# Query rotations, quantizer blocks and the last norm moved within a decoder kernel's order of work

## The chip, the cores and the metric

The kernel runs on one core of a Trainium2 chip. Its time is the device time of one execution in microseconds; the number used is the median of several executions. A core has a TensorE (PE) for matrix products and transposes, a VectorE (DVE), a ScalarE (ACT) and a GpSimd (POOL) for element-wise work, and SyncE (SP), which here only issues transfers. Each engine works through its own queue of instructions in order and waits on semaphores for what other engines produce. Data lies in on-chip SBUF; TensorE writes into PSUM, from which VectorE or ScalarE read.

## The reference

Two batches of 512 tokens, width 1024, with a context of 1024 rows each, go through two layers, each of an attention-like part and a feed-forward part. All is f32 except the first product, which is of integers.

```python
x = x + L0_xattn(layernorm(x), ctx)    # fake_quant(x) @ fake_quant(ctx): round, clip to 0..255
x = x + L0_ffn(layernorm(x))           # x @ W.T + b, plus LoRA terms weighted by a router's softmax
x = x + L1_xattn(layernorm(x), ctx)    # 32 query heads, 8 key/value heads of 128; rotary q and k;
                                       # softmax(q k / sqrt(128) + mask) v, then @ wo
x = x + L1_ffn(layernorm(x))           # x @ W_up.T, plus the LoRA term of the top-1 expert
```

The rotation of a query or a key is `q * cos + rotate_half(q) * sin`, where `rotate_half` swaps the two halves of the 128 channels with a sign. The top-1 expert is found by `argmax` over four logits.

## The kernel before

**Products.** Every large matrix product is split into two by two blocks and made from seven block products instead of eight (`seven` and `seven_onto`, L340 for their matmuls). The sums of blocks that this needs are made by `left_sums` and `right_sums` (L238 to L260), mostly on VectorE. A product of the seven is four or eight matmuls into one PSUM bank; it is then added to others (L277 copies the first on ScalarE; L281 to L293 add on VectorE; for sums onto x L308 to L315, with POOL doing L315). These functions are generators: one step is one block product.

**Order.** TensorE's instructions run in the order in which the program writes them. Other engines' instructions are ordered by a scheduler, except in hand-ordered regions: the very start on VectorE, and, from the first attention step to almost the last, VectorE, ScalarE and POOL. In the tail the scheduler orders them again. Buffers come from pools of 14, 17 and 10 slots of 8, 4 and 2 KB a partition (`u8`, `u4`, `u2`), with 2 wide PSUM buffers and 4 of one bank (`b`). Transfers are issued mostly from SP's queue, those of rows and some of the context from ScalarE's, constants from POOL's.

**First stage: keys and values, with the quantized product between.** For each batch, keys (two stages) and values (two stages) of 14 block products each are the main work. `quantized_product` (from L389 on) is woven in at every second block product (`weave`, called at L1035): it loads and quantizes eight context blocks two at a time, then for each of four row blocks of x makes the norm (L168, L175, L176), quantizes it (L193 to L197), and turns the block before it with eight bf16 transposes (`turned`, L406), evacuated by L158 or on ScalarE. Then come column sums (L427) and the four integer products (L441), evacuated by L449 and L451. Keys are rotated by `rope` (L210 to L216).

**Middle.** The first layer's linear part with its router, and the norm of x (`query_norm`, with transposes L203 evacuated by L204 and L205). Then the queries, eight stages of 14 block products; finished and rotated queries are stored to memory (`q_d`). The last stage's 14 products are not run at once: they are handed to attention as `extra["products"]`, spread over its first steps (3, 2, 2, 2, 2, 2, 1 at steps n = -2 to 4). Eight query heads come out of them. In this stage the list `later` collects whole rotations, and a step runs them at its end.

**Attention.** `attention` runs over n from -2; a step handles three heads in three stages of their life, and has three stretches. In the first the newest head's scores are made (L737, four pairs of matmuls into the wide buffers, evacuated with the mask added by L751 into `e`). In the second come the block products of the output projection of a former group, or the extra products, interleaved with the maximum tree of the newest head (L759 to L765). In the third, the middle head gets its maximum spread (L779), is reduced by it (L783), goes through the exponential (L786), and POOL sums it (L789 to L794); the oldest head is multiplied with the values (L800, copied by L808); and maxima and sums are turned by `over_partitions` (L701 transposes, L703 reduction, L774 reciprocal) and sent through memory to become rows (L710, L716). A head's output is divided by its sum on POOL (L811, in the next step).

**Tail.** During the last steps the moments of the first batch are taken (`all_moments`: L163, L164, square root L186, reciprocal L187), then that batch is normed and turned (`normed`, L168 and L203), the gate and the LoRA's inner product are made (`gated`: L929, the choice of the expert L940 to L952, transposes L962 and copy L963, L577), and the last linear layer runs (`linear`), first for batch 0 beside the last projection, then for batch 1. Its weight is loaded by L543 in four parts of 1 MB.

The lines that the change touches are L187, `rope`, the end of `quantized_product`, `finish` and `emit` in `queries`, the second and third stretch of `attention`, the `weave` of L1035 and the tail from L1128 on.

Of the kernel before, what the change touches and what calls it, by code (L numbers as in the profile page):

```python
# [31 lines left out]
NT = S // P  # L32
# [3 lines left out]
ATT_SCALE = float(np.float32(1.0) / np.sqrt(np.float32(DH)))  # L36
# [3 lines left out]
def decoder_kernel(  # L40
# [41 lines left out]
    def u4(shape, dtype=F32):  # L82
        return new(shape, "u4", 17, dtype)

    def u2(shape, dtype=F32):
        return new(shape, "u2", 10, dtype)
# [30 lines left out]
    for name, ap in qparams.items():  # L117
        t = const.tile([P, 1], F32, name=f"qp_{name}")
        nc.gpsimd.dma_start(t, ap.partition_broadcast(P))
        qp[name] = t  # L120
    for side in ("x1", "x2"):
        t = const.tile([P, 1], F32, name=f"qp_inv_{side}")
# [56 lines left out]
    def all_moments(b):  # L179

        mv, ready = small([P, NT, 2]), []
        for t in range(NT):
            moments(rows(b, t), mv[:, t, :])
            yield ready
        rstd = small([P, NT])
        nc.scalar.activation(rstd, mv[:, :, 1], AF.Sqrt, bias=eps_t)  # L186
        nc.vector.reciprocal(rstd, rstd)  # L187
        ready += [(mv[:, t, 0:1], rstd[:, t : t + 1]) for t in range(NT)]
        yield ready
# [16 lines left out]

    def rope(dst, acc, half, scale):

        rot = u2([P, HALF])
        nc.scalar.activation(rot[0:64, :], acc[64:128, :], AF.Copy, scale=scale)  # L210
        nc.scalar.activation(rot[64:128, :], acc[0:64, :], AF.Copy, scale=scale)
        nc.vector.scalar_tensor_tensor(
            dst, acc, scale, cos_t[half], ALU.mult, ALU.mult
        )
        nc.vector.tensor_tensor(rot, rot, sin_t[half], ALU.mult)
        nc.vector.tensor_tensor(dst, dst, rot, ALU.add)  # L216
# [111 lines left out]
    def weave(main, side, every, skip=0):  # L328

        for i, _ in enumerate(main):  # L330
            if i >= skip and (i - skip) % every == 0:
                next(side, None)

    def advance(stretches, n):
        for _ in range(n):
            next(stretches)
# [52 lines left out]
    def quantized_product(b):  # L389
        x[b] = halves()  # L390
        for t in range(NT):
            nc.sync.dma_start(rows(b, t), x_in[b, ts(t, P), :])
        q2 = [u8([P, 4, D], BF16) for _ in range(2)]
        for k in range(NKT):
            c_t = u4([P, D])
            nc.sync.dma_start(c_t, ctx_in[b, ts(k, P), :])
            quantized(q2[k // 4][:, k % 4, :], c_t, "x2")
            if k % 2:
                yield
        x1T = u8([P, NC, S], BF16)  # L400
        rsum, l1s = [], []

        def turned(t):
            tr = ps_wide().bitcast(BF16)[:, 0 : NC * P].rearrange("p (c n) -> p c n", c=NC)
            for c in range(NC):
                nc.tensor.transpose(tr[:, c, :], l1s[t][:, ts(c, P)], ident_b)  # L406
            copy_out(x1T[:, :, ts(t, P)], tr)

        for t in range(NT):
            h = layernorm(rows(b, t))  # L410
            l1 = u2([P, D], BF16)
            quantized(l1, h, "x1")
            r = small([P, 1])
            nc.scalar.activation(h, l1, AF.Copy, accum_out=r)
            nc.vector.tensor_scalar(r, r, c_x2, None, ALU.mult)
            rsum.append(r)
            l1s.append(l1)
            if t:
                turned(t - 1)
            yield  # L420
        turned(NT - 1)


        cs = ps_wide()
        for n in range(2):
            for k in range(NKT):
                nc.tensor.matmul(  # L427
                    cs[:, ts(n, HALF)],
                    ones_b,
                    q2[k // 4][:, k % 4, ts(n, HALF)],  # L430
                    start=(k == 0),
                    stop=(k == NKT - 1),
                )
        csum = u4([P, D])
        nc.vector.tensor_scalar(csum, cs, kc2, c_x1, ALU.add, ALU.mult)
        yield
        for t in range(NT):
            acc = ps_wide()
            for n in range(2):
                for c in range(NC):  # L440
                    nc.tensor.matmul(  # L441
                        acc[:, ts(n, HALF)],
                        x1T[:, c, ts(t, P)],
                        q2[c // 4][:, c % 4, ts(n, HALF)],
                        start=(c == 0),
                        stop=(c == NC - 1),
                    )
            y = u4([P, D])
            nc.vector.scalar_tensor_tensor(y, acc, rsum[t], csum, ALU.add, ALU.add)  # L449
            xs = rows(b, t)  # L450
            nc.vector.scalar_tensor_tensor(xs, y, s12, xs, ALU.mult, ALU.add)  # L451
            yield
# [187 lines left out]
    def queries(q, h_ops, w, later=None):  # L640

        def head(m):
            def product(i, acc, start):
                accumulate(
                    acc,
                    [(w[i - 1][:, c, ts(m, P)], h_ops[i - 1][:, c, :]) for c in range(4)],
                    start,
                )

            def finish(i, j, src):  # L650
                dst = u2([P, HALF]) if (i, j) == (0, 0) else src
                rope(dst, src, 0, ATT_SCALE)
                nc.sync.dma_start(q_d[j][4 * q + 2 * i + m], dst)

            def emit(i, j, src):
                if later is None:
                    finish(i, j, src)
                else:
                    later.append(lambda: finish(i, j, src))

            return seven(product, emit)

        return head(0), head(1)
# [161 lines left out]
    def attention(extra):  # L825
# [23 lines left out]
        for n in range(-2, total + GRP + 1):  # L849
# [27 lines left out]
            tree = new.tree() if new else iter(())  # L877
# [12 lines left out]
                next(tree, None)  # L890
            if n == GRP:
                w_ops = {i: output_operand(0, i) for i in (1, 6, 2, 7, 5, 4, 3)}
            for _ in tree:
                pass
            yield

            if mid:
# [13 lines left out]
                new.nmx = from_row(new.nmx)  # L911
            if old:
                old.attend(1)
            for act in extra["later"]:
                act()
            extra["later"].clear()
            yield


# [104 lines left out]
    side = chain(quantized_product(0), quantized_product(1))  # L1024
    for b in range(B):
        if b == 1:
            ctx_raw = [context_quarter(1, ch, kh, nc.scalar) for ch in range(2) for kh in range(2)]
            w = quad_weights(wk, 0)
            ctx_ops = context_sums(ctx_raw)
        for i, stage in enumerate((keys, keys, values, values)):  # L1030
            if b == 0 and i < 2:
                main = chain(*first[i])
            else:
                main = pair(*stage(b, i % 2, ctx_ops, w))
            weave(main, side, 2, 6 if b == 0 and i == 0 else 0)  # L1035
            if i < 3 and (b, i) != (0, 0):
                w = quad_weights((wk, wv)[(i + 1) // 2], (i + 1) % 2)
            if i == 1 and b == 1:
                for _ in side:
                    pass  # L1040
                ab_t = u8([P, 2, D])
                a_t, b_t = ab_t[:, 0].rearrange("p (c m) -> p c m", c=NC), ab_t[:, 1]
                nc.sync.dma_start(a_t, a0T.rearrange("(c p) m -> p c m", p=P))
                nc.gpsimd.dma_start(b_t, b0.partition_broadcast(P))  # L1044
                tT = [None] * B
                hs, steps = normed(0, u8, 2)
                side = chain(steps, routed(0, hs, a_t, b_t, tT))
# [35 lines left out]
    side = query_norm(1)  # L1083
# [29 lines left out]
    with tc.manual_schedule(  # L1113
        engines={
            mybir.EngineType.DVE,
            mybir.EngineType.Activation,
            mybir.EngineType.Pool,
        }
    ):
        for _ in range(3 * (B * NH - 5)):  # L1120
            next(steps)
        stats = all_moments(0)
        for _ in range(NT):
            for _ in range(2):
                next(steps)
            ready = next(stats)
            next(steps)
        next(stats)  # L1128
        for _ in range(3):
            next(steps)  # L1130

    hs, norms = normed(0, u4, 4, ready)
    for _ in range(6):
        next(norms, None)
        next(steps)
    gates = gated(hs)
    next(gates)
    for _ in range(2):
        next(steps)
    bl_t = u4([P, D])  # L1140
    nc.sync.dma_start(bl_t, bl1T)
    w_ops = matrix(wupT, u8, 4)
    zTs = [None, None]
    main = linear(0, token_sums(hs, lambda: u4([P, 4, 256])), w_ops, lambda: zTs[0], bl_t)
    advance(main, 2)
    zTs[0] = next(gates)
    advance(main, 2)
    for _ in range(3):
        next(steps)
    advance(main, 3)  # L1150
# [88 lines left out]
```

## Time and profile before

| | before |
|---|---|
| median of 3 executions | 2557.05 us (2554.49 to 2557.13) |
| the profiled execution | 2557.93 us |
| its span (first to last instruction) | 2556.2 us |
| mean granted TensorE clock | 0.979 |
| TensorE busy | 2455.1 us, 96% |
| VectorE busy | 1858.0 us, 73% |
| POOL busy | 997.6 us, 39% |
| ScalarE busy | 527.9 us, 21% |

The profile is of one execution. A group is named by its line, its engine, and its output and input buffers. A wait is written as the waiting line, an arrow, and the line that ended the wait. In a timeline a row has its start, its duration, the engine and line, and in brackets the idle time ahead of it with what ended it. A window row has the stretch, its length, and for each engine the busy time and the number of instructions, then the granted clock, the share of the transfer engines, and GB/s. One f32 matmul leaves two records.

### The profile page before, as it was taken

Reading aid. Unit: us, or ns where it says so; the run is one execution under the profiler, and the core shown is the slowest. Engines: PE = TensorE matmul, PEld = TensorE weight load, DVE = VectorE, ACT = ScalarE, POOL = GpSimd, SP = SyncE. Lnnn points to the kernel's source line nnn. Section 1 sums busy time; section 2 is a strip of 40 time slices with the busy share of each in tenths; the row PEclk is TensorE's granted clock in tenths of the full one; section 3 lists DMA queues with packets and bytes.
Section 4 is the critical chain, followed back from the end, with each engine's and each line's share of the span. In section 5 each row is a group of like instructions: output and inputs, shape, how many; then the busy total and the mean of one; then the engine's idle time right before and its main releaser. Section 6 shows DMA issues by size and latency. Waiting matters only on the chain. (4 is left out here: it accounts for less than half of the span.)

```text
span 2556.2 us, 19686 instructions
## 1 busy us (share of the span) xinstructions
PE 2455.1 (96%) x6848; PEld 1224.6 (48%) x6856; DVE 1858.0 (73%) x2036; ACT 527.9 (21%) x615; POOL 997.6 (39%) x536
## 2 busy tenths in 40 slices
PE   7999999999999997779999999999999999998998
PEld 3467458654444443334444444444444444444553
DVE  5848764346876555778888888888888888887542
ACT  1301121001222222122222222222222222222000
POOL 0000010110000001354767676767767676766221
PEclk8999999999999998889999999999999999999999
DMA  7325232013893221232343223442233224321300
GB/s 265 113 70 198 103 102 96 21 66 123 317 334 126 86 96 48 68 111 78 79 111 111 75 81 105 136 133 81 87 111 111 75 86 111 111 73 52 124 33 33
DMA packets 147379, 277.54 MB, mean 109 GB/s; under 512 B 29200, under 2 KB 47136, under 8 KB 146256
## 3 DMA queue, kind: packets, MB, share of 16 engines
q1 hardware_dynamic: 107024, 235.96, 28.0%
q10 hardware_dynamic: 39824, 39.60, 6.3%
q8 instruction: 55, 0.90, 0.2%
q0 software_dynamic: 432, 0.71, 0.1%
q14 instruction: 44, 0.36, 0.0%
HBM read 217.24 MB, written 58.98 MB: 108 GB/s over the span
## 5 line engine op out<-in xcount | busy, mean ns | idle before, releaser
L340 PE MATMUL b<-u,u 128*128 128x512 f32 (+1 forms) x3648 | 1415.5, 545 | 24.6 <-DVE u L284 9.6
L340 PEld LDWEIGHTS b<-u,u 128*128 128x128 f32 x3648 | 693.9, 192 | 710.9 <-issue 622.1
L737 PE MATMUL wide<-u,u 128*128 128x512 f32 x1024 | 469.7, 611 | 60.5 <-DVE u L751 58.6
L789 POOL TENSOR_TENSOR u<-u 128x1024 f32<-128x1024 f32 x64 | 151.6, 2368 | 796.3 <-ACT u L786 796.3
L800 PE MATMUL b<-u,u 128*128 128x512 f32 x1024 | 460.3, 592 | 0.0
L751 DVE TENSOR_TENSOR u<-wide,u 128x1024 f32<-128x1024 f32 x256 | 312.3, 1223 | 145.9 <-PE wide L737 145.9
L786 ACT ACTIVATE u<-u 128x2048 f32<-128x2048 f32 x128 | 244.6, 1911 | 788.6 <-DVE u L783 715.6
L737 PEld LDWEIGHTS wide<-u,u 128*128 128x128 f32 x1024 | 199.2, 196 | 319.6 <-issue 187.5
L783 DVE TENSOR_TENSOR u<-u,b 128x2048 f32<-128x2048 f32 x128 | 290.1, 2266 | 0.0
L800 PEld LDWEIGHTS b<-u,u 128*128 128x128 f32 x1024 | 186.2, 192 | 184.6 <-issue 184.6
L315 POOL TENSOR_TENSOR u<-u,u 128x512 f32<-128x512 f32 x120 | 186.9, 1577 | 223.4 <-DVE u L313 208.8
L313 DVE TENSOR_TENSOR u<-u,b 128x512 f32<-128x512 f32 x200 | 135.8, 679 | 135.3 <-PE b L340 135.2
L792 POOL TENSOR_TENSOR u<-u,u 128x1024 f32<-128x1024 f32 x64 | 150.8, 2356 | 37.7 <-ACT u L786 37.5
L793 POOL TENSOR_TENSOR u<-u,u 128x1024 f32<-128x1024 f32 x64 | 152.9, 2389 | 5.0
L811 POOL TENSOR_TENSOR u<-u,u 128x512 f32<-128x512 f32 x64 | 112.5, 1758 | 14.1 <-DMA u<-row 14.1
L1044 POOL DMA_DIRECT2D u<-in_b_dram x1 | 0.6, 561 | 287.5 <-PE wide L441 287.5
L759 DVE TENSOR_TENSOR u<-u 128x1024 f32<-128x1024 f32 x64 | 110.4, 1724 | 0.0
L210 ACT ACTIVATE u<-u 64x512 f32<-64x512 f32 x72 | 45.2, 628 | 313.7 <-DVE u L286 174.9
L701 PEld LDWEIGHTS wide<-ident,u 128*128 128x128 f32 x512 | 80.3, 203 | 61.6 <-issue 56.6
L761 DVE TENSOR_TENSOR u<-u,u 128x1024 f32<-128x1024 f32 x64 | 102.6, 1603 | 0.2
L794 POOL TENSOR_TENSOR u<-u 128x512 f32<-128x512 f32 x64 | 97.8, 1528 | 4.9
L703 DVE TENSOR_REDUCE small<-wide 128x4 f32<-128x512 f32 x128 | 87.2, 681 | 8.0 <-PE wide L701 8.0
(124 smaller groups left out, 1576.2 us busy)
## 6 DMA issues: line engine op xcount, KB each, us to landing
u<-row ACTq DMA_DIRECT2D x128, 256.0 KB, 3.6
u<-wo SPq DMA_DIRECT2D x64, 512.0 KB, 4.0
u<-in_wo_dram SPq DMA_DIRECT2D x48, 512.0 KB, 4.5
u<-in_wq_dram SPq DMA_DIRECT2D x32, 512.0 KB, 4.4
q<-u SPq DMA_DIRECT2D x64, 256.0 KB, 2.1
u<-in_wo_dram SPq DMA_DIRECT2D x16, 1024.0 KB, 7.4
wo<-u SPq DMA_DIRECT2D x32, 512.0 KB, 3.7
u<-q SPq DMA_DIRECT2D x64, 256.0 KB, 4.2
```

Of the source, the lines that this page charges most:

```text
L313: nc.vector.tensor_tensor(c, c, acc, ALU.add)
L315: nc.gpsimd.tensor_tensor(c, c, u, ALU.add)
L340: nc.tensor.matmul(acc, lhsT, rhs, start=start and k == 0, stop=k == len(pairs) - 1, skip_group_check=True,)
L737: nc.tensor.matmul(sc[:, ts(n, HALF)], self.kT[:, ts(2 * j + n, P)], self.qT, start=True, stop=True,)
L751: nc.vector.tensor_tensor(self.e[j // 2][:, js, :], sc.rearrange("p (k q) -> p k q", k=2), mask[j], ALU.add)
L783: nc.vector.tensor_tensor(e, e, self.nmf.unsqueeze(1).to_broadcast([P, 4, S]), ALU.add)
L786: nc.scalar.activation(e, e, AF.Exp)
L789: nc.gpsimd.tensor_tensor(d, e[:, 0:2, :], e[:, 2:4, :], ALU.add)
L792: nc.gpsimd.tensor_tensor(d, d, e[:, 0:2, :], ALU.add)
L793: nc.gpsimd.tensor_tensor(d, d, e[:, 2:4, :], ALU.add)
L800: nc.tensor.matmul(self.acc, self.v[:, k, :], self.e[j][:, k % 4, :], start=(k == 0), stop=(k == NKT - 1),)
L811: nc.gpsimd.tensor_tensor(self.oT, self.oT, self.den, ALU.mult)
```

## The change

Four moves within the order; no operation is added or taken away.

The rotation is split in two steps (`rope_steps`): the two copies on ScalarE, and the three operations on VectorE. For the last queries the copies are issued with their product, and the VectorE half, with the store of q, goes from the end of the attention step to behind the maximum tree of the same step. In the quantizer, block t - 2 is turned after block t has been quantized, not block t - 1, which gives the sequence one yield more, and the first `weave` starts at product 8 instead of 6. The reciprocal of the last norm's root gets a step of its own, taken one stretch later. In the tail, the norm's row blocks are in two `u8` tiles instead of eight `u4` quarters and are woven one by one between the stretches of the last attention steps in another pattern, and the second half of `gated` (L962, L963) comes ahead of the first products of `linear` instead of between them.

```diff
@@ all_moments
         nc.scalar.activation(rstd, mv[:, :, 1], AF.Sqrt, bias=eps_t)
+        yield ready
         nc.vector.reciprocal(rstd, rstd)
@@ rope
     def rope(dst, acc, half, scale):
 
+        for _ in rope_steps(dst, acc, half, scale):
+            pass
+
+    def rope_steps(dst, acc, half, scale):
+
         rot = u2([P, HALF])
         nc.scalar.activation(rot[0:64, :], acc[64:128, :], AF.Copy, scale=scale)
         nc.scalar.activation(rot[64:128, :], acc[0:64, :], AF.Copy, scale=scale)
+        yield
         nc.vector.scalar_tensor_tensor(
@@ quantized_product
             l1s.append(l1)
-            if t:
-                turned(t - 1)
-            yield
+            if t > 1:
+                turned(t - 2)
+            yield
+        turned(NT - 2)
+        yield
         turned(NT - 1)
@@ queries
             def finish(i, j, src):
                 dst = u2([P, HALF]) if (i, j) == (0, 0) else src
-                rope(dst, src, 0, ATT_SCALE)
+                yield from rope_steps(dst, src, 0, ATT_SCALE)
                 nc.sync.dma_start(q_d[j][4 * q + 2 * i + m], dst)
 
             def emit(i, j, src):
+                steps = finish(i, j, src)
+                next(steps)
                 if later is None:
-                    finish(i, j, src)
+                    next(steps, None)
                 else:
-                    later.append(lambda: finish(i, j, src))
+                    later.append(steps)
@@ attention, end of the second stretch
-            for _ in tree:
-                pass
+            for steps in (tree, *extra["later"]):
+                for _ in steps:
+                    pass
+            extra["later"].clear()
             yield
@@ attention, end of the third stretch
             if old:
                 old.attend(1)
-            for act in extra["later"]:
-                act()
-            extra["later"].clear()
             yield
@@ main
-            weave(main, side, 2, 6 if b == 0 and i == 0 else 0)
+            weave(main, side, 2, 8 if b == 0 and i == 0 else 0)
@@ tail
             ready = next(stats)
             next(steps)
+        next(steps)
         next(stats)
-        for _ in range(3):
+        next(steps)
+        next(stats)
+        hs, norms = normed(0, u8, 2, ready)
+        next(norms)
+        next(steps)
+
+    for _ in range(2):
+        next(steps)
+        for _ in range(2):
             next(steps)
-
-    hs, norms = normed(0, u4, 4, ready)
-    for _ in range(6):
-        next(norms, None)
-        next(steps)
+            next(norms)
     gates = gated(hs)
     next(gates)
     for _ in range(2):
         next(steps)
+    zTs = [next(gates), None]
     bl_t = u4([P, D])
     nc.sync.dma_start(bl_t, bl1T)
     w_ops = matrix(wupT, u8, 4)
-    zTs = [None, None]
     main = linear(0, token_sums(hs, lambda: u4([P, 4, 256])), w_ops, lambda: zTs[0], bl_t)
-    advance(main, 2)
-    zTs[0] = next(gates)
-    advance(main, 2)
+    advance(main, 4)
```

## The prediction

> **What bounds the kernel now.** I read the engine table and the 40 slices first, then TensorE's waits, then the stretches where its share falls, then the queues inside one of them.
>
> ```profile
> PE 2455.1 (96%) x6848; PEld 1224.6 (48%) x6856; DVE 1858.0 (73%) x2036; ACT 527.9 (21%) x615; POOL 997.6 (39%) x536
> PE   7999999999999997779999999999999999998998
> PEclk8999999999999998889999999999999999999999
> ```
>
> TensorE sets the time; it falls short in slice 1, slices 16 to 18 and near the end, and its clock falls in the same places. Only there can an order gain anything. Its waits:
>
> ```profile
> PE wide L737 <- DVE u L751: 58.6, 11, 11.6
> PE b L340 <- DVE u L284: 9.6, 3, 6.1
> PE wide L406 <- DVE u L197: 5.6, 3, 4.6
> PE wide L203 <- DVE u L168: 2.9, 1, 2.9
> PE b L340 <- DVE u L963: 2.9, 1, 2.9
> ```
>
> (total, times, longest.) The scores L737 have two wide PSUM buffers, so the third and fourth matmul pair of a head wait until VectorE's L751 has evacuated the first. Of the 58.6 us, 51.7 lie between 940 and 1170 (seven waits) and 5.6 at 2319. The busy times by 20 us place it: one ramp step, and the steady phase after it:
>
> ```profile
> 1080.00:1100.00 20.00, 20.00 (x54) 9.42 (x53) 15.46 (x14) 5.00 (x4) 9.57 (x5) 1.00 0.29 75
> 1100.00:1120.00 20.00, 10.27 (x27) 4.47 (x25) 15.46 (x11) 7.29 (x8) 13.64 (x7) 0.85 0.17 40
> 1200.00:2300.00 1100.00, 1097.02 (x2855) 509.75 (x2854) 959.50 (x855) 275.65 (x239) 777.25 (x394) 1.00 0.35 100
> ```
>
> (PE, PEld, DVE, ACT, POOL, clock, DMA.) From 1160 on TensorE is full, so all that can be won in attention is in the eight query rotations of the ramp. VectorE's, ScalarE's and TensorE's order around the worst stall:
>
> ```profile
> 1104.04 2.28 DVE L783 TENSOR_TENSOR u<-u,b 128x2048 f32<-128x2048 f32 x1
> 1110.06 1.25 DVE L212 SCALAR_TENSOR_TENSOR u<-u,cos_t 128x512 f32<-128x512 f32 x1 [3.74 <-ACT u L211]
> 1111.23 2.82 DVE L215 TENSOR_TENSOR u<-u,sin_t 128x512 f32<-128x512 f32 x1
> 1120.65 2.34 DVE L751 TENSOR_TENSOR u<-wide,u 128x1024 f32<-128x1024 f32 x2
> 1106.35 1.91 ACT L786 ACTIVATE u<-u 128x2048 f32<-128x2048 f32 x1 [1.67 <-DVE u L783]
> 1108.76 0.63 ACT L210 ACTIVATE u<-u 64x512 f32<-64x512 f32 x1
> 1121.91 6.47 PE L737 MATMUL wide<-u,u 128*128 128x512 f32 x8 [11.65 <-DVE u L751]
> ```
>
> The rotation's copies L210 queue behind the exponentials, its VectorE half waits for them, and the next head's L751 stands behind all of it, ready since about 1108.6.
>
> **What the Trainium skill says.** "TensorE: Matmul & The Clock Gate", Part 1, says that an idle window of about 3.4 us halves TensorE's clock until one busy window has passed. The trace agrees: 8 records of L737 take 3.60 us ahead of the stall and 6.47 behind it. So each stall over about 3 us costs some 2.5 to 3 more. "GPSIMD Engine Reference", 1. Specifications, says that GpSimd shares its SBUF interfaces with VectorE instructions of two SBUF inputs. L215 takes 0.69 us elsewhere (101.10), 2.82 here, where POOL adds. "ScalarE activation tables: per-element evaluation and per-set limits", What a function is on this engine, gives 1283 ns for a table load; the trace has 1.28 at 2321.97, ahead of the square root.
>
> **Part 1, rotations.** Nothing is removed. Two copies (2 × 0.63 us, ScalarE) go from behind the exponentials to right behind their product; L212, L215, L216 and the store of q go from the step's end to behind the tree (L759 to L765), ahead of the sum's L703. The step now ends with L783, and L751 follows it at once. The q stores reach SP's queue one stretch earlier, ahead of the next head's loads; they take 2.1 us to land and their readers come much later, so I cost them at nothing. ScalarE is idle when the copies now come (11.76 us of waiting ahead of the exponential at 1102.77). POOL has finished its sums at that point of the step, so I take 1.93 us for a rotation (0.69 + 0.69 + 0.69, less overlap), 4.6 beside POOL at worst.
>
> From one step's first L340 to the next's, n = -2 to 4, the trace has 25.7, 27.6, 30.8, 34.0, 21.5, 36.2, 28.3 us. TensorE's own work at full clock (a record of 128x512 issues every 0.43 us; scores 6.9, attend 6.9, each turn 0.47, each product 3.4) is 17.6, 14.1, 21.4, 21.4, 21.4, 21.4, 18.0. The difference is 8.1, 13.5, 9.4, 12.6, 0.1, 14.8, 10.3, together 68.8. The step without rotations (n = 2) loses 0.1 with the same tree, exponentials and scores: this is the control.
>
> After the change VectorE's work in these steps (four L751 4.7, tree 4.4, 0.6 per product's addition, 1.93 per rotation, L703 and L774 0.7 to 1.5, two L783 4.45) is 11.7, 16.8, 18.2, 20.1, 16.3, 20.1, 17.6. It is under TensorE's except for n = -1. What stays: n = -2 about 1.8 (its maximum is turned 2.5 us later); n = -1 about 6.5 (2.7 of VectorE's excess, the rest the maximum's way through memory, with too little TensorE work to cover it); n = 1 and 3, with two rotations, 1.5 each: at n = 2 L783 ends at 1084.78 and the first L751 is due at 1087.11, 2.3 us of slack against 3.9 of rotation; the others 0.1 to 1, together 1.6. That is 12.9, a gain of 55.9; I take 55, from 45 to 60.
>
> **Part 2, quantizer.** L406 (8 transposes, 0.6 us) of a row block is issued one yield, two products of 3.4 us, later, and the sequence starts two products later. Now it waits 0.35, 4.64 and 0.6 us for L197, with a cold clock behind the long one (L427), about 9 us together from 120 to 160. VectorE's last three L197 end at 112.0, 123.2, 135.4; TensorE passes the new places at about 122, 129, 137 and the last at 144, and the four L238 to L246 (4.9 us, 127.61) stand earlier in the new order, so the blocks are ready at about 119, 134 and 139 for the last three against 129, 137 and 144. Gain 8, from 3 to 9. In the second batch the 0.75 us wait of L406 at 248 goes, and loads reordered on SP may cost up to 1: -1 to +1. Near 335 (L284 behind L168, 2.85 us and a cold clock) the order stays alike; I take 0, from -3 to +3.
>
> **Part 3, reciprocal.** L187 waits 4.85 us for the square root behind L786, L808 and the table load, L751 behind it, TensorE 5.61. Behind the next tree it waits for nothing. The products would start about 2323.5 instead of 2330.48: -7.
>
> **Part 4, gate and last norm.** The last norm's row blocks are interleaved with the last heads' products two by two, in u8 tiles, and L962 with its z moves ahead of the next linear's first products a1, b1. Two waits are new. L701 of head 62 comes without scores ahead of it, and its L794 stands behind L811 and two L315 on POOL: I estimate it at 2352.6 instead of 2356.61, but with 7.7 us of idle TensorE and a cold clock in front, and L929 at 2376.7 instead of 2378.19. So of the 7 only 1.5 are left. Then L962 needs the last L952 (now at 2402.29, behind the gate's small instructions, the token sums and L252); a1 and b1 covered it, now TensorE waits about 6.5 us there and runs cold. In return L963 no longer delays a2 (2.87 us). a2 ends at about 2414.3 instead of 2411.0. L260 comes late in VectorE's order through the u8 slots: +1. Behind L701 stand the last attends, and with them two of the loads of the last weight, whose u8 slots they free: issued at some 2375 and landing 10.4 us later (the median of these four now), still ahead of L255's need, so at no cost. The tail: +3 in all, from -7 to +8.
>
> **Sum.** -55 - 8 - 0.5 + 3 = -60.5. The span of 2556.2 becomes 2495.7; the profiled execution took 2557.93, 1.7 more than its span, and the median is 0.9 below it: 2496.5 us.
>
> **Rivals.** (a) VectorE becomes the bound in the ramp: two rotations beside POOL at 4.6 us each add 5.3 us at n = 1 and 3, 2.7 at the others, and stalls past 3 us bring the cold clock back. The slow 2.82 us at 1111.23 speaks for it, the idle POOL behind the tree against it. Ramp gain 25 to 42: 2510 to 2527. (b) The tail keeps the reciprocal's 7 us and its new waits are hidden, because the scheduler's small instructions run sooner than I count: 2482 to 2489. For it speaks that VectorE is idle 5.84 us at 2378.39; against it, L952's place. (c) Slower: the rotation stands ahead of the sum's L703 and both L783, so a late copy L211 holds VectorE and with it the denominator, the exponentials and the next scores. This would happen if the copies got stuck behind the previous step's two L786 and L808 (4.4 us) and their row loads. It decides from 61 / 7 = 8.7 us per step on; at 10 us the time is 2566. Against it: these ended at 1087.6, and n = 3's products run from 1091.99. (d) The gain is not there, because another wait stands right behind L751: the step n = 2 excludes it.
>
> **How the numbers follow.** As summed 0.58, with its own range 2487 to 2507; (a) 0.24; (b) 0.11; (c) 0.05, (d) 0.02. The range of 2483 to 2521 leaves out (c), (d), the upper part of (a) and the best end of (b). 0.2% (5 us) is what a measurement tells from no change. Faster 0.93, same 0.02, slower 0.05.
>
> **What would show it.** Right: from 960 to 1160 hardly any L737 waiting for L751, granted clock near 1, steady attention beginning some 63 us earlier; L406 without waits for L197. Part 4 right: TensorE idle ahead of L701 and L962 some 60 us earlier than 2345 and 2394. Wrong: L212 waiting for L211 inside the new place, rotations of 4 us, or a wait of L340 for L163 to L197 in the keys stage.

## The result, and the profile after

The changed kernel takes 2508.95 us (median of 4, 2505.61 to 2512.61), the kernel before on the same footing 2555.77 (4 runs): a ratio of 0.9818, 95% interval 0.9801 to 0.9835. It is faster by 47 us; 2496.5 was forecast, so the time lies 12.5 us above the forecast and inside its range (2483 to 2521).

Lines have moved. In the kernel after, and in the runs made from it, the products L340 are L347, the scores L737 are L748, the evacuation L751 is L762, the tree L759 to L765 is L770 to L776, the turns L701 are L712, the reductions L703 are L714, L783 is L794, the exponential L786 is L797, POOL's sums of exponentials L789 to L794 are L800 to L805, the division L811 is L822, the product with the values L800 is L811. The rotation's copies L210 and L211 are L216 and L217, its VectorE half L212 to L216 is L219 to L223. The quantizer's transposes L406 are L413, the norm's L203 are L204, the gate's L962 and L963 are L972 and L973, and L952, which makes z, is now L962. The block sums L238 to L246 are L245 to L253, and L315 is L322.

The page of the kernel after, engine table and slices:

```profile
PE 2441.2 (97%) x6848; PEld 1218.0 (49%) x6856; DVE 1851.0 (74%) x2036; ACT 527.7 (21%) x615; POOL 1006.5 (40%) x536
PE   7999999999999998989999999999999999998998
PEclk8999999999999999999999999999999999999899
```

TensorE's dip in slices 16 to 18 is almost filled, and its clock stays full there. TensorE's waits after (total, times, longest):

```profile
PE wide L712 <- POOL u L805: 8.5, 3, 6.8
PE wide L748 <- DVE small L714: 8.5, 5, 3.3
PE wide L748 <- DVE u L762: 8.3, 9, 1.6
PE b L972 <- DVE u L962: 5.9, 3, 3.2
```

The scores' waits for evacuation have fallen from 58.6 us to 8.3. No wait for the quantized blocks is left. Three waits have grown or are new: L712 for POOL's sums (0.4 us before), the scores for the reductions L714 (1.4 before), and L972 for z (none before). Each turned row block stands behind its products without a bracket, in TensorE's order after:

```profile
129.04 0.61 PE L413 MATMUL wide<-ident_b,u 128*128 128x128 bf16 x8
129.49 7.13 PE L347 MATMUL b<-u,u 128*128 128x256 f32 x32
136.45 0.61 PE L413 MATMUL wide<-ident_b,u 128*128 128x128 bf16 x8
```

Read at the same landmarks of both traces, the profiled executions differ like this (step n = -2 starts at 952.45 before and 944.53 after, n = 5 at 1156.51 and 1100.69):

| stretch (us) | before | after | difference | forecast |
|---|---|---|---|---|
| start to the first product of step n = -2 | 952.45 | 944.53 | -7.9 | -8.5 |
| ramp, n = -2 to n = 5 | 204.06 | 156.16 | -47.9 | -55 |
| n = 5 to the end of the span | 1399.69 | 1403.11 | +3.4 | +3 |
| span | 2556.2 | 2503.8 | -52.4 | -60.5 |

So 8.1 of the 12.5 us are missing in the span, all but 1 of them in the ramp. The remaining 4.4 come from how the span was carried over to a median: the profiled execution, 2505.61, is the fastest of the four and 3.3 below their median, where before it was 0.9 above its own.

The ramp's steps, each less TensorE's own work as the prediction counted it:

| n | -2 | -1 | 0 | 1 | 2 | 3 | 4 | sum |
|---|---|---|---|---|---|---|---|---|
| before | 8.1 | 13.5 | 9.4 | 12.6 | 0.1 | 14.8 | 10.3 | 68.8 |
| forecast | 1.8 | 6.5 | 0.1 to 1 | 1.5 | 0.1 | 1.5 | 0.1 to 1 | 12.9 |
| after | 2.1 | 5.4 | 1.2 | 2.7 | 0.1 | 1.8 | 7.6 | 20.9 |

Almost all of the miss is one step, n = 4. VectorE's queue there, after (start, duration, line, idle time ahead):

```profile
1075.31 1.23 DVE L762 TENSOR_TENSOR u<-wide,u 128x1024 f32<-128x1024 f32 x1 [0.49 <-PE wide L748]
1076.45 2.34 DVE L770 TENSOR_TENSOR u<-u 128x1024 f32<-128x1024 f32 x1
1078.83 2.17 DVE L772 TENSOR_TENSOR u<-u,u 128x1024 f32<-128x1024 f32 x1
1081.03 2.17 DVE L774 TENSOR_TENSOR u<-u,u 128x1024 f32<-128x1024 f32 x1
1083.24 1.63 DVE L776 TENSOR_TENSOR u<-u 128x512 f32<-128x512 f32 x1
1084.79 0.68 DVE L300 TENSOR_TENSOR u<-u,b 128x512 f32<-128x512 f32 x1
1086.86 0.92 DVE L219 SCALAR_TENSOR_TENSOR u<-u,cos_t 128x512 f32<-128x512 f32 x1 [1.40 <-ACT u L217]
1087.71 1.75 DVE L222 TENSOR_TENSOR u<-u,sin_t 128x512 f32<-128x512 f32 x1
1089.49 0.69 DVE L223 TENSOR_TENSOR u<-u,u 128x512 f32<-128x512 f32 x1
```

and POOL's queue in the same stretch:

```profile
1075.36 2.35 POOL L804 TENSOR_TENSOR u<-u,u 128x1024 f32<-128x1024 f32 x1
1077.79 2.13 POOL L805 TENSOR_TENSOR u<-u 128x512 f32<-128x512 f32 x1
1079.88 2.24 POOL L822 TENSOR_TENSOR u<-u,u 128x512 f32<-128x512 f32 x1
1082.20 2.12 POOL L245 TENSOR_TENSOR u<-u 128x512 f32<-128x512 f32 x1
1084.40 1.60 POOL L248 TENSOR_TENSOR u<-u,u 128x512 f32<-128x512 f32 x1
1085.97 1.27 POOL L250 TENSOR_TENSOR u<-u 128x512 f32<-128x512 f32 x1
1087.20 1.71 POOL L253 TENSOR_TENSOR u<-u,u 128x512 f32<-128x512 f32 x1
```

The tree takes 8.3 us, where before it took 4.4, beside POOL operations of 128x512, of which five in six also take 1.6 to 2.2 us instead of the 1.26 they have alone. The rotation takes 3.4 instead of the 1.9 counted for it. TensorE pays for it in five waits: 1.26 us for L805, 0.86 for the tree's end L776, 1.67 and 1.00 for the reductions L714 behind the rotation, and 1.34 for L762. Before, the tree of the same step, and POOL's work ahead of it and behind it, looked like this:

```profile
1130.81 1.23 DVE L761 TENSOR_TENSOR u<-u,u 128x1024 f32<-128x1024 f32 x1
...
1121.81 1.27 POOL L246 TENSOR_TENSOR u<-u,u 128x512 f32<-128x512 f32 x1
1139.63 2.37 POOL L789 TENSOR_TENSOR u<-u 128x1024 f32<-128x1024 f32 x1 [16.55 <-ACT u L786]
```

TensorE's stall of 11.65 us ended at 1121.91, POOL had finished its block sums about a microsecond later, at 1123.08, and the tree ran alone. Once the stall is gone, the step's parts close up and POOL's work of the step before comes to lie beside the tree.

This happens in other steps too: the tree's four operations take 5.9, 6.9, 6.9, 6.1 and 8.3 us at n = 0 to 4. With these trees, and the slowed rotation at n = 4, the prediction's count of VectorE's work becomes an estimate of 19.7, 22.6, 18.8, 21.8 and 22.9 us, against 21.4 us of TensorE's own work in the first four steps and 18.0 at n = 4. So n = 4 is over by about 5 us, n = 1 by about 1, n = 3 by 0.4, the others not at all. Two things set n = 4 apart. It has one product and not two, so the forecast left it 0.4 us of room. And POOL makes four block sums in it, L245 to L253, for the projection of the first group, which no other step of the ramp has. No run takes these four alone away.

### The profile page after: what moved, and what is told of

The parts are those of the page before. It is cut to its first block, busy times and chain, and to the rows that moved or that the text cites. A ratio compares the mean times of both kernels' runs of the same rounds, so it can differ in the third digit from the quotient of the medians.

```text
span 2503.8 us, 19692 instructions
## 1 busy us (share of the span) xinstructions
PE 2441.2 (97%) x6848; PEld 1218.0 (49%) x6856; DVE 1851.0 (74%) x2036; ACT 527.7 (21%) x615; POOL 1006.5 (40%) x536
## 5 line engine op out<-in xcount | busy, mean ns | idle before, releaser
L347 PE MATMUL b<-u,u 128*128 128x512 f32 (+1 forms) x3648 | 1416.6, 546 | 23.5 <-DVE u L291 10.0
L347 PEld LDWEIGHTS b<-u,u 128*128 128x128 f32 x3648 | 694.2, 192 | 710.8 <-issue 623.6
L748 PE MATMUL wide<-u,u 128*128 128x512 f32 x1024 | 455.3, 595 | 17.2 <-DVE small L714 8.5
L811 PE MATMUL b<-u,u 128*128 128x512 f32 x1024 | 461.3, 593 | 0.0
L800 POOL TENSOR_TENSOR u<-u 128x1024 f32<-128x1024 f32 x64 | 151.5, 2367 | 735.8 <-DMA row<-small 383.9
L762 DVE TENSOR_TENSOR u<-wide,u 128x1024 f32<-128x1024 f32 x256 | 312.7, 1224 | 129.0 <-PE wide L748 129.0
L797 ACT ACTIVATE u<-u 128x2048 f32<-128x2048 f32 x128 | 244.7, 1912 | 695.3 <-DVE u L794 633.9
L748 PEld LDWEIGHTS wide<-u,u 128*128 128x128 f32 x1024 | 193.0, 190 | 268.3 <-issue 175.4
L794 DVE TENSOR_TENSOR u<-u,b 128x2048 f32<-128x2048 f32 x128 | 290.3, 2268 | 0.0
L322 POOL TENSOR_TENSOR u<-u,u 128x512 f32<-128x512 f32 x120 | 185.5, 1564 | 228.3 <-DVE u L320 213.5
L811 PEld LDWEIGHTS b<-u,u 128*128 128x128 f32 x1024 | 186.7, 192 | 185.2 <-issue 185.2
L804 POOL TENSOR_TENSOR u<-u,u 128x1024 f32<-128x1024 f32 x64 | 150.8, 2356 | 4.9
L822 POOL TENSOR_TENSOR u<-u,u 128x512 f32<-128x512 f32 x64 | 119.8, 1871 | 16.0 <-DMA u<-row 16.0
L216 ACT ACTIVATE u<-u 64x512 f32<-64x512 f32 x72 | 45.2, 628 | 343.2 <-DVE u L293 166.9
L770 DVE TENSOR_TENSOR u<-u 128x1024 f32<-128x1024 f32 x64 | 115.6, 1806 | 0.0
L712 PEld LDWEIGHTS wide<-ident,u 128*128 128x128 f32 x512 | 80.4, 203 | 70.9 <-issue 56.6
L772 DVE TENSOR_TENSOR u<-u,u 128x1024 f32<-128x1024 f32 x64 | 105.8, 1654 | 0.2
L805 POOL TENSOR_TENSOR u<-u 128x512 f32<-128x512 f32 x64 | 100.2, 1566 | 4.9
L774 DVE TENSOR_TENSOR u<-u,u 128x1024 f32<-128x1024 f32 x64 | 97.0, 1515 | 0.2
```

The costliest lines, as they stand in the source:

```text
L322: nc.gpsimd.tensor_tensor(c, c, u, ALU.add)
L347: nc.tensor.matmul(acc, lhsT, rhs, start=start and k == 0, stop=k == len(pairs) - 1, skip_group_check=True,)
L748: nc.tensor.matmul(sc[:, ts(n, HALF)], self.kT[:, ts(2 * j + n, P)], self.qT, start=True, stop=True,)
L762: nc.vector.tensor_tensor(self.e[j // 2][:, js, :], sc.rearrange("p (k q) -> p k q", k=2), mask[j], ALU.add)
L794: nc.vector.tensor_tensor(e, e, self.nmf.unsqueeze(1).to_broadcast([P, 4, S]), ALU.add)
L797: nc.scalar.activation(e, e, AF.Exp)
```

## The experiments

**The parts one by one.** Each is the kernel before with one part of the diff shown above; the reciprocal alone also needs its two `next(stats)` in two stretches:

```diff
+        next(steps)
         next(stats)
-        for _ in range(3):
-            next(steps)
+        next(steps)
+        next(stats)
+        next(steps)
```

> Before, with the rotations' part alone (copies with their product, VectorE's half behind the tree). Theory: nearly the whole gain is made in the ramp, and the parts add up. From the two traces, the ramp from n = -2 to n = 5 is 47.9 us shorter after, so about 2508 (ratio 0.981), with the quantizer's waits for L197 and the stall at the root as before. Rival: the ramp's gain needs the other parts (a shifted state of queues and transfers): under 35 us, above 2520.

Measured 2509.82 us, ratio 0.9821 (0.9805 to 0.9838). As the theory said: the rotations alone make the gain, and their ramp shows the same seven numbers as the full change within 0.1 us (2.1, 5.3, 1.3, 2.7, 0.1, 1.8, 7.7).

> Before, with the quantizer's part alone. Theory: -8 us, as the start of the ramp stands 7.9 us earlier in the trace after: about 2548 (ratio 0.997), TensorE without waits for the quantized blocks between 100 and 160 us. Rival: the gain is absorbed by the loads of the second batch's keys or by a wait behind: -3 or less, 2553 or more.

Measured 2552.58, ratio 0.9978 (0.9968 to 0.9988): -5.6 us by the medians. In its trace the start of the ramp is 8.9 us earlier than before, and its turned blocks stand without a wait. So the waits went as the theory said. On its size the times don't decide well: the interval is -8.2 to -3.1 us, which takes in the theory's -8 and ends just short of the rival's -3.

> Before, with the root and its reciprocal taken apart, the reciprocal behind the next tree; norm and gate as before. Theory: L751 no longer stands behind the reciprocal, so the stall of 5.6 us with its cold clock goes and 5 to 7 us are gained: about 2550 (ratio 0.9975). Rival: the wait comes back at the next step's end, because L168 now waits for the reciprocal: 0 to -2 us, 2554 or more.

Measured 2551.92, ratio 0.9979 (0.9970 to 0.9988), -6.2 us: the theory.

> Before, with everything that changes in the tail (reciprocal, norm in u8 tiles woven otherwise, gate's transposes ahead of the linear's first products). Theory: the trace after loses 3.4 us between n = 5 and the end, so about 2559 (ratio 1.0013): the waits of L701 for POOL's sums and of L962 for z take more than the reciprocal gives. Rival: it gains alone, and the loss seen in the trace after lies in steady attention: 2550 or less.

Measured 2563.59, ratio 1.0023 (1.0012 to 1.0034), +5.4 us: slower, as the theory said. Since the reciprocal alone gives 6.2, norm and gate cost 11.7. The parts -48.3, -5.6 and +5.4 add up to -48.5; the whole change measures -46.8. So they add up within about 2 us.

**The ramp.** Where VectorE's half goes, with the copies early:

```diff
-            for steps in (tree, *extra["later"]):
-                for _ in steps:
-                    pass
-            extra["later"].clear()
+            for _ in tree:
+                pass
             yield
...
             if old:
                 old.attend(1)
+            for steps in extra["later"]:
+                for _ in steps:
+                    pass
+            extra["later"].clear()
             yield
```

> The changed kernel with the copies issued with their product, but VectorE's half of the rotations left at the end of the step. Theory: both halves of the edit matter; the copies remove VectorE's wait of about 3.7 us for L211, but the rotation still runs beside POOL (4 to 5.7 us instead of 1.9) and ahead of the next L751: the ramp gains about half, and the time is 2528 to 2538. Rival: the copies behind the exponentials were the whole cost: within 5 us of the changed kernel, about 2510. Other rival: only the place on VectorE counts: 2545 or more.

Measured 2536.79, ratio 0.9922 (0.9908 to 0.9936). VectorE at the end of its step n = 3:

```profile
1080.74 2.28 DVE L794 TENSOR_TENSOR u<-u,b 128x2048 f32<-128x2048 f32 x1
1082.93 2.23 DVE L219 SCALAR_TENSOR_TENSOR u<-u,cos_t 128x512 f32<-128x512 f32 x1
1085.09 0.68 DVE L222 TENSOR_TENSOR u<-u,sin_t 128x512 f32<-128x512 f32 x1
1085.81 2.71 DVE L223 TENSOR_TENSOR u<-u,u 128x512 f32<-128x512 f32 x1
```

No wait for the copies is left, but the three operations take 5.6 us beside POOL's sums, ahead of the next evacuation. The ramp is 20.1 us shorter than before, of the 47.9 of the full change: the early copies alone give less than half of the gain, and the place on VectorE the rest. The new place with late copies was not run.

POOL's work taken out of the ramp:

```diff
+            if not self.b and self.hd < 6:
+                if j == 0:
+                    self.d = u4([P, 2, S])
+                    nc.gpsimd.memset(self.d, 1.0)
-            if j == 0:
+            elif j == 0:
...
-            nc.gpsimd.tensor_tensor(self.oT, self.oT, self.den, ALU.mult)
+            if self.b or self.hd > 3:
+                nc.gpsimd.tensor_tensor(self.oT, self.oT, self.den, ALU.mult)
...
+                if n == GRP:
+                    o_ops = [quarters[i] for i in (0, 1, 0, 3, 1, 3, 2)]
+                else:
+                    o_ops = left_sums(nc.gpsimd, *quarters, lambda: sums[:, next(places)])
```

> The changed kernel without POOL's work in the ramp: the sums of the first six heads' exponentials (a memset takes their place), the divisions of the first four and the first group's block sums are left out. Now the steps n = -2 to 4 lose 20.9 us against TensorE's own work, 7.6 of them at n = 4. Theory: POOL's additions stretch the tree (8.3 us instead of 4.4 at n = 4) and the last rotation (3.4 instead of 1.9), and this is what the forecast of the ramp missed: n = 4 falls to 2 us or less, all steps to 11 to 14 us, and the tree's operations take 1.23 us. Rival: the loss is the order on VectorE and the maximum's way through memory: n = 4 stays above 5 us, all steps above 18.

One execution, 2500.33 us. The steps lose 2.1, 7.7, 0.2, 0.7, 0.1, 0.7 and 2.3 us, 14.0 together against the 12.9 that had been forecast. Its VectorE queue at n = 4:

```profile
1075.64 1.23 DVE L772 TENSOR_TENSOR u<-u,u 128x1024 f32<-128x1024 f32 x1
1076.90 1.23 DVE L774 TENSOR_TENSOR u<-u,u 128x1024 f32<-128x1024 f32 x1
1078.16 0.69 DVE L776 TENSOR_TENSOR u<-u 128x512 f32<-128x512 f32 x1
1078.77 0.68 DVE L300 TENSOR_TENSOR u<-u,b 128x512 f32<-128x512 f32 x1
1080.84 0.69 DVE L219 SCALAR_TENSOR_TENSOR u<-u,cos_t 128x512 f32<-128x512 f32 x1 [1.39 <-ACT u L217]
```

The tree is back at 4.4 us and n = 4 at the theory's figure; the wait of 1.4 us for the copies is unchanged, so it was not the cause. The run also takes away L712's wait for POOL's sums (1.26 us at n = 4), so up to that much of the 5.3 gained at n = 4 is not the sharing itself. n = -1 is not better (7.7; it lies between 5.3 and 7.7 in all runs with rotations in the new place and two products there): in all of them the scores wait 3.3 us for L714, which stands on VectorE behind the rotation and L794.

The rotations left out:

```diff
             def finish(i, j, src):
                 dst = u2([P, HALF]) if (i, j) == (0, 0) else src
-                yield from rope_steps(dst, src, 0, ATT_SCALE)
+                if later is None:
+                    yield from rope_steps(dst, src, 0, ATT_SCALE)
+                else:
+                    if (i, j) == (0, 0):
+                        nc.scalar.copy(dst, src)
+                    yield
```

> The changed kernel without the rotation of the last eight heads' queries (the products are stored as they are, one of two first copied out). Theory: in their new place the rotations cost almost nothing except at n = 4, where the last one stands late: the ramp is 3 to 6 us shorter, most of it at n = 4. Rival: the rotations still hold VectorE up in each step: 10 us or more.

One execution, 2494.87 us. The steps lose 0.0, 3.4, 0.1, 0.1, 0.2, 0.1 and 2.0 us, 6.1 together. The expectation of 3 to 6 us missed: the rotations still cost 14.8 us (20.9 - 6.1), more than the rival's 10, even where they stand now. Of it 5.6 is at n = 4; the rest, 2.1, 2.0, 1.0, 2.6 and 1.6, is at n = -2, -1, 0, 1 and 3. At n = 4 the tree is slowed in this run too (two of its operations take 2.18 and 2.17 us), and yet only 2.0 are lost there. So the 5 to 6 us at n = 4 need both: POOL beside VectorE, and a rotation behind the slowed tree. Either one alone nearly fits into the step: it loses 2.0 to 2.3 us.

The addition earlier at n = 4, on the kernel with the tail as before (below):

```diff
-            for _ in range(3 + k % 2):
+            for _ in range(2 if n == GRP else 3 + k % 2):
                 next(stretches, None)
                 next(tree, None)
```

> The kernel with rotations, quantizer and reciprocal, norm and gate as before, and at n = 4 the extra product's addition ahead of the last two operations of the tree instead of behind it. Theory: the addition no longer waits behind the slowed tree, the copies on ScalarE run under its second half, and VectorE's wait of 1.4 us for them goes: 1 to 3 us less than 2494.6. Rival: n = 4 is bound by POOL's sums, on which the turn of the denominator waits: the same within 1 us.

Measured 2497.58, ratio 0.9770 (0.9757 to 0.9784), against 0.9770 (0.9756 to 0.9785) without the edit: no difference, and n = 4 loses 7.4 us, as ever. The wait for the copies is gone, but its VectorE queue shows what came instead:

```profile
1088.16 1.75 DVE L219 SCALAR_TENSOR_TENSOR u<-u,cos_t 128x512 f32<-128x512 f32 x1
1089.84 1.75 DVE L222 TENSOR_TENSOR u<-u,sin_t 128x512 f32<-128x512 f32 x1
1091.62 1.64 DVE L223 TENSOR_TENSOR u<-u,u 128x512 f32<-128x512 f32 x1
```

The rotation, earlier against POOL's queue, now lies wholly beside POOL's block sums: 5.1 us. The theory missed: what the addition saved, the rotation lost. The rival got the number right; its reason, L712's wait for the sums, is 1.38 us of the 7.4.

**The tail.** The changed kernel with norm and gate as before, and with L972 alone put back:

```diff
-    zTs = [next(gates), None]
+    zTs = [None, None]
...
-    advance(main, 4)
+    advance(main, 2)
+    zTs[0] = next(gates)
+    advance(main, 2)
```

> The changed kernel with norm and gate in the tail as before (rotations, quantizer and reciprocal kept). Theory: parts add up, so -48.3 - 5.6 - 6.2 = -60 against before: about 2498 (ratio 0.9765), 10 us below the changed kernel. Rival: the changed tail's loss depends on the other parts; 2505 or more.

Measured 2494.61, ratio 0.9770 (0.9756 to 0.9785), the fastest median of all runs. It is 14 us below the changed kernel by the medians and 12 by the two ratios, whose intervals leave room for the 10 expected.

> The changed kernel with the gate's transposes L962 back behind the linear's first two products (norm in u8 and its weaving kept). Theory: of the changed tail's loss against the reciprocal alone (about 12 us) the wait for z is one half, 5.9 us of idle time and the cold clock after it, less some 3 us for the second product's wait on zT: 4 to 6 us gained, about 2504. Rival: the wait only moves to the second product: 2508 to 2510.

Measured 2499.99, ratio 0.9779 (0.9766 to 0.9792), 9 us below the changed kernel by the medians, more than the 4 to 6 expected. With a1 and b1 ahead of it, L972 waits for nothing, and the product behind it waits 1.04 us for zT. The wait of L712 stays. What the norm's new weaving costs by itself, the difference between this run and the one ahead of it, is too small to tell: their intervals overlap. TensorE in the tail of the changed kernel:

```profile
2294.89 1.13 PE L712 MATMUL wide<-ident,u 128*128 128x128 f32 x4 [6.79 <-POOL u L805]
...
2338.24 0.33 PE L972 MATMUL b<-ident,u 128*128 128x128 f32 x1 [1.75 <-DVE u L962]
2341.74 0.48 PE L972 MATMUL b<-ident,u 128*128 128x128 f32 x1 [3.18 <-DVE u L962]
```

and POOL ahead of the first of these waits:

```profile
2285.27 1.26 POOL L322 TENSOR_TENSOR u<-u,u 128x512 f32<-128x512 f32 x1 [1.23 <-DVE u L320]
2286.49 2.36 POOL L803 TENSOR_TENSOR u<-u,u 128x1024 f32<-128x1024 f32 x1
2288.81 1.26 POOL L322 TENSOR_TENSOR u<-u,u 128x512 f32<-128x512 f32 x1
2290.04 2.36 POOL L804 TENSOR_TENSOR u<-u,u 128x1024 f32<-128x1024 f32 x1
2292.35 1.26 POOL L822 TENSOR_TENSOR u<-u,u 128x512 f32<-128x512 f32 x1
2293.57 1.26 POOL L805 TENSOR_TENSOR u<-u 128x512 f32<-128x512 f32 x1
```

**A better ramp.** A product moved from n = 4 to n = -1, on the kernel with the tail as before:

```diff
-    extra = {-2: 3, -1: 2, 0: 2, 1: 2, 2: 2, 3: 2, 4: 1}
+    extra = {-2: 3, -1: 3, 0: 2, 1: 2, 2: 2, 3: 2}
```

> As the one with the tail as before, and one of the extra products moved from step n = 4 to n = -1 (3, 3, 2, 2, 2, 2, 0). Theory: n = -1 wastes 5.4 us for want of TensorE's work, so its third product is nearly free (up to 3.4 us), and n = 4 loses its product and its rotation, which stand behind a tree slowed by POOL: 4 to 7 us less than without the shift, about 2492. Rival: the stall of n = 4 only goes to n = 3 or to the first step of the projection: within 2 us of 2498.

Measured 2500.88, ratio 0.9782 (0.9769 to 0.9795): not faster, but 6 us slower by the medians, with intervals that overlap. TensorE's order at n = 4:

```profile
1078.15 3.70 PE L748 MATMUL wide<-u,u 128*128 128x512 f32 x8 [1.35 <-DVE u L762]
1086.14 1.13 PE L712 MATMUL wide<-ident,u 128*128 128x128 f32 x4 [4.29 <-POOL u L805]
1087.06 4.65 PE L811 MATMUL b<-u,u 128*128 128x512 f32 x8
```

Without a product, nothing covers POOL's sums: the turn waits 4.29 us, and the eight records behind it take 4.65 us instead of 3.60. The stall stayed in its step and took another cause. At n = -1 the third product was not nearly free either: the step takes 24.2 us, where it took 20.6 with two products, so it grew by 3.7 for a product of 3.4. In both the scores wait 3.3 us for L714, for L714 stands behind the last product's rotation on VectorE and moved with it. Of the 6 us only 1.0 lies in the ramp by the two traces; the rest was not traced to a cause.

At most one rotation a step, none at n = 4, and the first row block of the last norm scaled before the exponentials:

```diff
-            for steps in (tree, *extra["later"]):
-                for _ in steps:
-                    pass
-            extra["later"].clear()
+            for _ in tree:
+                pass
+            if n != GRP:
+                for steps in extra["later"][:1]:
+                    for _ in steps:
+                        pass
+                del extra["later"][:1]
...
         next(stats)
+        hs, norms = normed(0, u4, 4, ready)
+        next(norms)
         next(steps)
 
-    hs, norms = normed(0, u4, 4, ready)
-    for _ in range(6):
-        next(norms, None)
+    for i in range(6):
+        if i:
+            next(norms, None)
         next(steps)
```

> The kernel with rotations, quantizer and reciprocal, norm and gate as before, with two more edits. VectorE's half of a rotation: at most one a step and none at n = 4 (one at each of n = -2 to 3, 5 and 6); and the last norm's first row block is scaled ahead of the step's exponentials. Theory: at n = 4 the loss needs POOL's sums and the rotation together (7.6 us with both, 2.3 and 2.0 without one), so it falls to about 2, n = 1 from 2.7 to 1 or less, against 1 to 3 us at n = 2, 5 and 6, where the tree is slowed too; the wait of L203 for L168 (3.5 us and the clock after it) goes: 6 to 10 us less than 2494.6, about 2487. Rival: VectorE has no room for a rotation beside POOL in any full step, and what n = 4 wins is lost at n = 5 and 6: 2491 to 2496.

Measured 2496.28, ratio 0.9760 (0.9740 to 0.9779): no difference from 0.9770, and not the 2487 of the theory. In its trace the ramp to n = 5 loses 15.0 us instead of 21.0 (n = 4 falls from 7.3 to 4.1, n = 1 and n = 3 to 0.8 and 0.7), but 3.7 of these 6.0 us come back at n = 5 and 6, as the rival said; and the wait of 3.5 us of L204 for L168 is replaced by one of 3.5 us of L712 for POOL's sums in the same place. The executions spread from 2489.32 to 2503.58, so a gain of a few us can't be told.

## Why the prediction was right, and where it was off

**Where the bound lies.** Right. 51.7 us of waits in the ramp and their cold clock were what could be won there; steady attention is untouched (TensorE is busy 1097.7 us of 1100 after, 1097.0 before).

**Part 1, rotations.** The mechanism was right in both halves, and the control step n = 2 was a sound reason to expect no further wait behind L751: it loses 0.1 us in every run that gives it no rotation. Forecast 55, measured 47.9 in the traces. The term that was mis-sized is VectorE's work at n = 4, "tree 4.4" and "1.93 per rotation": they measured 8.3 and 3.4. The step behind it was "POOL has finished its sums at that point of the step": it was read from a trace in which a stall stood between POOL's sums and the tree. "SBUF — State Buffer" of the Trainium skill, Who interferes with whom, says that a VectorE instruction with two SBUF inputs contends with a GpSimd instruction that reads SBUF, and that one with at most one SBUF input, outside the two-port modes, does not. The traces agree: the tree's operations of two SBUF inputs go from 1.23 to 2.17 us, while L762 (PSUM and SBUF) stays at 1.23 beside L804. The prediction counted with this sharing for the rotation only, and not for the tree. Without POOL's work the ramp is 6.9 us shorter, of which up to 1.3 at n = 4 is the wait of L712 for its sums.

The forecast of 6.5 us for n = -1 came near (5.4) with a reason that holds only in part. VectorE does hold this step up, but "too little TensorE work to cover it" was not the limit: one more product there only made the step longer.

**Rival (a)** was this contention, but at n = 1 and 3, where two rotations come together. There the rotations themselves ran undisturbed (0.69 us an operation); the slowed tree cost these steps 1.2 and 0.3 us more than forecast. It decided at n = 4 alone, and the ramp fell 7.1 us short of the forecast, where the rival had 13 to 30.

**Part 2, quantizer.** Right: the blocks are ready, the waits are gone, and the ramp starts 7.9 us earlier where 8.5 were forecast. By the medians of the part alone the gain is 5.6, in the range of 3 to 9.

**Part 3, reciprocal.** Right: -6.2 against -7.

**Part 4, tail.** Right in both new waits: L712 6.79 us (7.7 forecast), with two L322 and L822 ahead of L805 on POOL as argued (3.8 us of work; no run moves them alone), L972 5.9 us (6.5), and +3.4 for the whole tail (+3). Rival (b), that they would be hidden, fell: the tail alone is slower by 0.12 to 0.34%.

**Rival (c)** did not come in its size. The copies stand behind nothing long on ScalarE. VectorE's longest wait for them in the ramp is 6.0 us, at n = -2, where their product has only just ended. The reduction L714 stands behind the rotation there, and TensorE waits 1.81 us for it, the 1.8 that the forecast had for this step. At n = 4 the wait is 1.4 us. **(d)** fell with the run of the rotations alone.

## What to carry to other kernels

A stall in a queue keeps other engines apart. Before costing what is left after a stall is removed, slide the other queues together and ask which of their operations come to lie beside each other; durations read next to a stall are durations without neighbours. And a move that gains by itself may carry another that loses: here the parts added up, and leaving out the one that lost gave 2494.6 us instead of 2509.0.

## What was not expected of the hardware

Sharing is paid twice: beside POOL, a 128x1024 f32 operation of two SBUF inputs on VectorE takes 2.17 to 2.34 us instead of 1.23, and most of POOL's 128x512 operations 1.6 to 2.25 instead of 1.26. Yet POOL's work without the rotation, or the rotation without POOL's work, costs step n = 4 about 2 us, both together 7.6. What stays open is the spread: the executions of one program lie 7 us apart for the changed kernel (4 executions), 14 for the one with a rotation a step (5) and 10 for the kernel before (23), and a single trace does not show where.
